# Layer 2's context product in two terms instead of three, and the image columns taken from a wider value product

## The chip, the cores and the metric

The kernel runs on one core of a Trainium2 chip, as one launch. The metric is the device time of one execution in microseconds; the time of a version is the median of its runs. Matrix products run on TensorE (PE), which reads SBUF and writes to PSUM, eight banks of 128 x 512 floats. VectorE (DVE), ScalarE (ACT) and GpSimd (POOL) do the elementwise work, each with a queue of its own that is worked off in order. SyncE (SP) issues most of the transfers, ScalarE some.

## The reference

Two attention layers follow each other on a sequence of 16 batches x 256 positions x 320 channels, 20 heads of 16 channels. Each layer has a context of 256 tokens x 512 channels; the last four tokens are image tokens. Layer 2 is the one that matters here (252 text tokens, 4 image tokens):

```
probs_t  = softmax(q k_t^T * scale)                # text attention, b h s t
text_out = probs_t v_t
qsem     = probs_t @ text_ehs                      # b h s e, 512 wide
qsem     = qsem / max(|qsem|, 1e-12)
ip_n     = ip_ehs / max(|ip_ehs|, 1e-12)
sem      = qsem @ ip_n^T                           # b h s 4
probs_ip = softmax((q k_ip^T) * scale + 0.5*sem) * spatial_mask
out      = (text_out + probs_ip v_ip) @ W_out + b_out + residual
```

The 512 wide `qsem` is never formed. With the context c of a batch, the length of `qsem` is p^T (c c^T) p for a row p of probabilities, and its product with an image token is p^T (c c_image^T). So per batch the kernel needs the product of the context with itself (252 x 252) and of the context with its four image columns.

## The kernel before, in words

**Numbers in two halves.** TensorE's operands are rounded (`float32r`). Where more accuracy is wanted, a value is stored as a high half (rounded) and a low half (the rest), and `prod` (L205) adds three products for each of four 128-channel slices: high by high, high by low, low by high. That is 12 matrix products for one result. `ct(s, k)` is slice k of a batch's context, s = 0 high, s = 1 low, in the buffers `cta`; ScalarE makes the high half and GpSimd the low half (both in `halves`, L147 and L148).

**Layers and slots.** Layer 1 takes slots 0 to 79, layer 2 slots 80 to 159, five slots (groups of four heads) for each batch; a slot of layer 2 takes about 11 us. `slot1` writes out the fixed work of a slot: scores for the maxima (`S`, L780), turned scores (`T`, L775) and their exponentials (`P`, L788), ScalarE's halved and rounded copy of P (`ctb`, L806), GpSimd's remainder (`wt`, L807), the product of the context blocks with the rounded probabilities (`norm1`, L816, bank `X`), VectorE's product of that with the remainder (L817), and `attend1` (L825 with the values `v1t`, L828 with the sums for the length). `settle1` (L870 to L874) turns the result on VectorE.

**Tasks between the fixed work.** Everything that is done once a batch is a generator. `task` gives it due times in slots, and `fill` runs the next step of whichever task is due first, at three points of a slot (0.33, 0.67, 1.0). For batch b, with n = 80 + 5b:
- `keys1` (k1, n-7 to n-4.67): loads the context, makes its halves, and the keys.
- `tokens1` (t1, n-3.67, n-3, n-2.67, n-2.33): two value products of 320 columns (`wC`), then two context products of 256 columns. Text tokens are covered by two tiles of 128 that overlap by four; t = 0 is the first tile, t = 1 starts at token 124 (`DUP`), and `tmask` zeroes the four duplicates.
- `open1` (o1): splits the residual (`hq`, L517 to L519), queries (L528, L536, L537), their product with the image keys.
- `image_softmax` (i1): the softmax over the image tokens, small steps that alternate between GpSimd, VectorE and ScalarE. It begins with a power on GpSimd (L894); `z` (L912) and `rs` (L914) end it, and VectorE turns `rs` (L921).
- `close1` (c1): three image products (L931), added on VectorE (L932), the split `ho`, the output projection (L528).

`tokens1` fills two things: `v1t`, for each head 16 value columns, a column of ones and four image columns (17 to 20), and `G`, seven blocks of 128 x 128 for `norm1`: block 0 is the high half of tile 0 by tile 0 and block 4 its remainder, block 1 the high half of tile 0 by tile 1, blocks 2, 5, 3 and 6 what tile 1 gives. `norm1` adds blocks 0, 2, 4, 5 for the first result and 1, 3, 6 for the second; block 5 is doubled ahead of that (L495).

**What sets the order.** TensorE's instructions stand in the order in which the code issues them. Those of the other engines are ordered by the build's own scheduler, so a change in one step can reorder them around it. PSUM: `X` banks serve `prod`, `norm1`, the maxima and the projections in turn, and a product that needs a bank waits until the engine that reads it out is done. `buf` gives SBUF buffers from fixed rings by name.

Of the kernel before, what the change touches and what calls it, by code (L numbers as in the profile page):

```python
# [9 lines left out]
FR = mybir.dt.float32r  # L10
# [8 lines left out]
H = 20  # L19
# [29 lines left out]
def xattn2(  # L49
# [39 lines left out]
    def bank(tag="X"):  # L89
        return ps.tile([128, 512], F32, tag=tag, name=tag, bufs=BANKS[tag])  # L90
# [3 lines left out]
        return ps.tile([128, 1024], F32, tag="S", name="S", bufs=1).rearrange("p (h t) -> p h t", h=4)  # L94


    words, slots = {"ctb": 1024, "cta": 1024, "raw": 512, "rawc": 512, "kb": 1152, "si": 256, "mt": S, "mx": 2, "kst": 4 * S, "rs": 2 * S, "P": 4 * S}, {}

    def buf(tag, shape, dtype=F32, bufs=1, name=None):
        if tag in ("wB", "wD", "vr", "raw"):  # L100
# [308 lines left out]

    def weights6():  # L410
        cip = w1["cip"]
        w1["v"] = yield from weights(wv1_d, "wC", None, 0.3, "rawc")
        wvi1 = yield from weights_by_column(wvi1_d, 0.3, "rawc")
        vip = buf("rawc", [128, 512], bufs=2, name="vip")[:BI, :CP]
        for m in range(3):
            ms = slice(m * 128, m * 128 + 128)
            vp = bank()[:BI, :128]
            prod(vp, lambda s, k: cip[:, s, k], lambda s, k: wvi1(s, k, ms), 4)
            nc.vector.tensor_copy(vip[:, ms], vp)
            yield  # L420
        ind1 = buf("M", [2, 2, S], FR, bufs=SIZES["M"], name="ind")
        nc.scalar.activation(ind1, ident[:2, :2].unsqueeze(2).to_broadcast([2, 2, S]), AF.Copy, scale=-1.0)
        w1["ind"] = ind1
        dma(kmask, kmask_d.rearrange("(m p) c -> p m c", p=128))
        dma(vipd, vip)
        for i in range(2):
            v = buf("wD", [128, 2, 640], bufs=2, name="v1t")
            nc.gpsimd.memset(v, 0.0)
            nc.vector.memset(vcols(v, V1W)[:, 0, :, 16], 1.0)
            nc.vector.tensor_scalar_add(vcols(v, V1W)[:, 1, :, 16], vcols(v, V1W)[:, 1, :, 16], tmask[:, 2:3])  # L430
            v1t.append(v)
        yield
# [17 lines left out]
            nc.vector.memset(w1["mhalf"], -0.5)  # L450
            nc.gpsimd.memset(w1["pip"], 0.0)

    ct1 = {}

    def keys1(b):
        ct = ct1[b] = yield from context(b, 1, 0.3)
        for m in range(3):
            ms = slice(m * 128, (m + 1) * 128)
            kst = buf("kst", [128, 2, 2, S], FR, bufs=SIZES["KST"]).rearrange("p s b t -> p (s b t)")
            kst = kst[:, : 2 * S].rearrange("p (s b t) -> p s b t", s=2, b=1)  # L460
            kp = bank()[:, :T1]
            prod(kp, lambda s, k: w1["k"](s, k, ms), lambda s, k: ct(s, k)[:, :T1], 4)
            halves(kst[:, 0, 0, :T1], kst[:, 1, 0, :T1], kp)
            nc.gpsimd.tensor_copy(kst[:, :, 0, T1:], f(kip[:, :, m, 4 * b : 4 * b + 4]))
            keys_out(kd[1][b], m, kst)
            yield

    def tokens1(b):
        ct = ct1[b]
        V, G = v1t[b % 2], gmt[b % 2]  # L470
        vc = vcols(V, V1W)
        for t, lo, sc in ((0, 0, 1.0), (1, DUP, tmask[:, 2:3])):
            vp = bank()[:, :320]
            prod(vp, lambda s, k: ct(s, k)[:, lo : lo + 128], w1["v"], 4)
            nc.scalar.activation(vc[:, t, :, 0:16], vp.rearrange("p (h d) -> p h d", d=D), AF.Copy, scale=sc)
            yield
        rnb = rn[:, 4 * b : 4 * b + 4].unsqueeze(1).to_broadcast([128, H, NIP])
        for t, lo in ((0, 0), (1, DUP)):
            g = bank()[:, :S]
            prod(g, lambda s, k: ct(s, k)[:, lo : lo + 128], ct, 4)  # L480
            ip = g[:, T1:S].unsqueeze(1).to_broadcast([128, H, NIP])
            if t == 0:
                nc.vector.tensor_mul(vc[:, 0, :, 17:21], ip, rnb)
                nc.scalar.copy(G[:, 0, :], g[:, 0:128])
                nc.scalar.copy(G[:, 1, 4:], g[:, 128:T1])
                nc.vector.tensor_sub(G[:, 4, :], g[:, 0:128], f(G[:, 0, :]))
            else:
                tm = tmask[:, 2:3]
                nc.vector.scalar_tensor_tensor(vc[:, 1, :, 17:21], ip, tm, rnb, op0=ALU.mult, op1=ALU.mult)
# [5 lines left out]
                nc.vector.tensor_scalar_mul(G[:, 5, :], f(G[:, 5, :]), 2.0)  # L495
                nc.vector.scalar_tensor_tensor(
                    G[:, 6, 4:], g[:, 128:T1], tm, f(G[:, 3, 4:]), op0=ALU.mult, op1=ALU.subtract
                )
            yield
        return V, G  # L500

# [520 lines left out]
    for b in range(B):  # L1022
        n = NS + 5 * b
        task(("k1", b), shifted(n, -7, -6.67, -6.33, -5.67, -5, -4.67), lambda b=b: keys1(b), ("w2",), *([("t1", b - 1)] if b else []), *([("w4", 1)] if b > 2 else []))
        task(("t1", b), shifted(n, -3.67, -3, -2.67, -2.33), lambda b=b: tokens1(b), ("k1", b), ("w3", b % 2))
# [159 lines left out]
```

## Time and profile before

| | us |
|---|---|
| median of 3 runs | 1624.44 |
| lowest, highest | 1620.82, 1625.23 |
| span of the profiled execution, first to last instruction | 1631.7 |
| a batch of layer 2 in the profile | 55.0 |

| engine | busy us | share of the span |
|---|---|---|
| TensorE, products | 1540.0 | 94% |
| TensorE, weight loads (beside the products) | 1235.5 | 76% |
| VectorE | 1215.7 | 75% |
| GpSimd | 1188.4 | 73% |
| ScalarE | 828.8 | 51% |

The profile is one execution with the hardware profiler. No other time is given for it than its span, which is 7.3 us longer than the median of the runs. A row of the timeline has the start, the duration of the group (or of its members together), engine, line, operation, output and inputs, the shape and, in brackets, the engine's idle time before it and what ended it. Products of TensorE are pipelined: the duration of a group runs to the end of its last one, and the next group starts before that, so the cost of a group is the distance to the next start.

### The profile page before, as it was taken

To read this page: it belongs to the slowest core of one execution; us is meant where nothing else is said; L and a number is where in the kernel's file an instruction comes from. 1 tells how busy PE (TensorE), PEld (TensorE's weight loads), DVE (VectorE), ACT (ScalarE), POOL (GpSimd) and SP (SyncE) were. 2 spreads that over 40 slices of the span, in tenths; PEclk is the share of its full clock that TensorE was granted. 3 is DMA by queue.
4 is the path that set the end of the run, shared out by engine and by line. 5 is a ranking of instruction groups with operands and counts; after the bars stand their busy time and mean duration, and the time that the engine had idled before them with its cause. 6 is when DMAs were issued, how large, how long until landed. Compare 5 with 4: busy or idle time off the path is not lost.

```text
span 1631.7 us, 36363 instructions
## 1 busy us (share of the span) xinstructions
PE 1540.0 (94%) x13306; PEld 1235.5 (76%) x13306; DVE 1215.7 (75%) x2410; ACT 828.8 (51%) x1797; POOL 1188.4 (73%) x1147
## 2 busy tenths in 40 slices
PE   7899999999999899789999999999999999999996
PEld 6777878788878787577777777777777777777765
DVE  5467777677777677868877787878777887777785
ACT  5344545445454545435555555545554555555462
POOL 3358787878787867767688668766876787678776
PEclk9799999999999999799999999999999999999998
DMA  7767676667777675666424332433344243423301
GB/s 219 201 202 205 202 203 202 190 207 199 208 199 207 177 210 165 162 191 178 144 74 130 114 125 89 133 120 112 101 126 128 88 125 114 139 81 106 112 26 44
DMA packets 235741, 243.06 MB, mean 149 GB/s; under 512 B 19050, under 2 KB 219468, under 8 KB 235564
## 3 DMA queue, kind: packets, MB, share of 16 engines
q1 hardware_dynamic: 233356, 239.44, 49.8%
q8 instruction: 106, 1.74, 0.5%
q10 hardware_dynamic: 2208, 1.30, 0.3%
q14 instruction: 71, 0.58, 0.1%
HBM read 116.78 MB, written 88.18 MB: 126 GB/s over the span
## 4 chain that ended last, share of the span: by engine, by line
PE 55%; DVE 13%; DMA 10%; POOL 9%; ACT 4%; issue 3%; SPq 3%; ACTq 0%; POOLq 0%; DVEq 0%
PE X L205 15%; PE X L816 12%; PE X L528 7%; PE P L709 5%; PE P L825 3%; DMA qs<-mt 3%; POOL P L682 3%; PE S L652 3%; PE P L828 3%; DMA qs<-qd 3%; PE T L775 3%; SPq L82 2%; PE T L676 2%; DVE wt L817 2%; DVE ho L518 2%
## 5 line engine op out<-in xcount | busy, mean ns | idle before, releaser
L682 POOL TENSOR_TENSOR P<-P,rs 128x512 f32<-128x512 f32 x320 | 413.4, 1313 | 159.5 <-ACT P L679 159.2
L807 POOL TENSOR_TENSOR wt<-P,ctb 128x512 f32<-128x512 f32 x320 | 422.3, 1335 | 93.0 <-ACT ctb L806 91.3
L816 PE MATMUL X<-ctb,gm 128*128 128x512 f32 x1120 | 330.4, 413 | 2.1 <-DVE wt L817 1.1
L679 ACT ACTIVATE P<-T 128x512 f32<-128x512 f32 x320 | 176.1, 595 | 222.1 <-PE T L676 111.8
L806 ACT ACTIVATE ctb<-P 128x512 fp32r<-128x512 f32 x320 | 195.6, 631 | 98.3 <-PE X L816 91.5
L816 PEld LDWEIGHTS X<-ctb,gm 128*128 128x128 f32 x1120 | 189.2, 188 | 72.3 <-issue 15.6
L817 DVE TENSOR_TENSOR wt<-X,wt 128x512 f32<-128x512 f32 x320 | 218.2, 683 | 33.9 <-PE X L816 28.4
L781 DVE TENSOR_REDUCE mn<-S 128x4 fp32r<-128x1008 f32 x160 | 191.8, 1199 | 48.3 <-PE S L780 48.2
L788 ACT ACTIVATE P<-T 128x512 f32<-128x512 f32 x320 | 173.7, 595 | 64.3 <-PE P L825 48.3
L654 DVE TENSOR_REDUCE mn<-S 128x4 fp32r<-128x716 f32 x160 | 142.5, 891 | 0.0
L709 PE MATMUL P<-P,vr 128*32 128x256 f32 x1920 | 132.1, 409 | 3.3 <-DVE mx L581 2.3
L676 PE MATMUL T<-qs,ks 127*128 127x256 f32 x640 | 112.3, 295 | 22.6 <-DMA qs<-mt 10.7
L652 PE MATMUL S<-ks,qs 125*128 125x256 f32 x640 | 118.4, 309 | 3.7 <-DVE mn L654 2.5
L652 PEld LDWEIGHTS S<-ks,qs 125*128 125x128 f32 x640 | 89.3, 196 | 40.6 <-issue 35.0
L528 PE MATMUL X<-ho,wF 128*128 128x256 f32 x768 | 112.8, 290 | 6.3 <-DVE ho L518 3.0
L528 PE MATMUL X<-hq,wE 128*128 128x256 f32 x768 | 111.5, 289 | 7.1 <-ACT hq L517 3.3
L894 POOL TENSOR_TENSOR r<-u,rs 128x40 f32<-128x40 f32 (+2 forms) x17 | 108.7, 6393 | 7.7 <-DVE u L891 7.6
L676 PEld LDWEIGHTS T<-qs,ks 127*128 127x128 f32 x640 | 92.8, 198 | 28.0 <-DVE tmp L726 11.6
L528 PEld LDWEIGHTS X<-ho,wF 128*128 128x128 f32 x768 | 103.2, 194 | 12.6 <-DVE ho L518 4.7
L528 PEld LDWEIGHTS X<-hq,wE 128*128 128x128 f32 x768 | 103.5, 195 | 11.7 <-ACT hq L517 3.7
L205 PE MATMUL X<-cta,wA 128*128 128x252 f32 (+1 forms) x720 | 100.9, 286 | 7.3 <-ACT wA L147 5.7
L205 PEld LDWEIGHTS X<-cta,wA 128*128 128x128 f32 x720 | 94.1, 195 | 12.5 <-ACT wA L147 5.9
(197 smaller groups left out, 2813.6 us busy)
## 6 DMA issues: line engine op xcount, KB each, us to landing
qd<-q SPq DMA_DIRECT2D x96, 384.0 KB
qs<-tph SPq DMA_DIRECT2D x64, 308.0 KB
kd<-kst SPq DMA_DIRECT2D x73, 256.0 KB
rawc<-in_cT_dram SPq DMA_DIRECT2D x60, 256.0 KB
qs<-qd SPq DMA_DIRECT2D x80, 192.0 KB
ks<-kd SPq DMA_DIRECT2D x80, 192.0 KB
ks<-kd SPq DMA_DIRECT2D x160, 96.0 KB
qs<-qd SPq DMA_DIRECT2D x160, 96.0 KB
```

The lines of the kernel that those rows point to most:

```text
L205: last = mm(out, lhs(a, k), rhs(b, k), start=i == 0, stop=i == len(terms) - 1)
L528: mm(pp, w(s, k, slice(m * 128, (m + 1) * 128)), a[:, t], start=i == 0, stop=i == len(terms) - 1)
L652: mm(sp[:, h], Q[: XROW + T0, h, t * 128 : (t + 1) * 128], K[: XROW + T0, h], start=True, stop=True)
L676: mm(st[p][:, j], K[:KS0, 2 * p + j, t * 128 : (t + 1) * 128], Q[:KS0, 2 * p + j], start=True, stop=True)
L679: exp = anchor(nc.scalar.activation(pt, st[p], AF.Exp, scale=SCALE))
L682: anchor(nc.gpsimd.tensor_mul(pt, pt, rs[:, t : t + 1].to_broadcast([128, 2, S])))
L709: mm(pv[32 * s : 32 * s + 32, o : o + S], v[:, vt, h : h + 32], P[k, s // 2][:, t, s % 2], start=vt < 2, stop=vt != 1,)
L781: anchor(nc.vector.tensor_reduce(maxes[k + 2][:, t], sp[:, :, :T1], axis=AX.X, op=ALU.max))
L806: nc.scalar.activation(R[k, u][:, t], P[k, u][:, t], AF.Copy, scale=0.5)
L807: anchor(nc.gpsimd.tensor_sub(W[k, u][:, t], P[k, u][:, t], f(R[k, u][:, t])))
L816: mm(yp, gm[:, gb], R[k, u][:, kt], start=i == 0, stop=i == len(blocks[n]) - 1)
L817: nc.vector.tensor_mul(W[k, u][:, n], yp, W[k, u][:, n])
```

## The change

- The context product becomes two terms. For each slice the stationary operand is the high half in both; the moving operands are the high half and the doubled low half, 252 columns. That is 8 products instead of 12 for each of the two tiles. Twice high by low is not symmetric, but p^T (A + A^T) p = 2 p^T A p.
- The doubled low halves (`two`, in buffers `tph`) are made on ScalarE at the end of `keys1`, four instructions of 128 x 252.
- The image columns come from the value product: `wC` has four more columns for each slice and half, which GpSimd fills with the image columns of the context (four copies of 128 x 8 a batch). The value products have 324 columns, and the two VectorE products for columns 17 to 20 of `v1t` move to the value steps.
- Of tile 0 by tile 1 the remainder is kept (`across`, VectorE), turned on TensorE in a fifth step of `tokens1`, due at n-2, into free columns of the bank of the second context product, and added to block 5 (VectorE). Block 5's doubling goes.

```diff
 def weights6():
-        w1["v"] = yield from weights(wv1_d, "wC", None, 0.3, "rawc")
+        wv = w1["wv"] = buf("wC", [128, 2, 4, H * D + NIP], FR)
+        parts = [(wv1_d[k * 128 : (k + 1) * 128], wv[:, 0, k, : H * D], wv[:, 1, k, : H * D]) for k in range(4)]
+        yield from in_turn(parts, 0.3, "rawc")
...
 def keys1(b):
...
+        two = [buf("tph", [128, 2, S], FR, bufs=2, name="two") for i in range(2)]
+        twice = doubled[b] = lambda k: two[k // 2][:, k % 2, :T1]
+        for k in range(4):
+            nc.gpsimd.tensor_copy(wv[:, :, k, H * D :], f(ct(slice(None), k)[:, :, T1:]))
+        for k in range(4):
+            nc.scalar.activation(twice(k), f(ct(1, k)[:, :T1]), AF.Copy, scale=2.0)
+        yield
...
 def tokens1(b):
-            vp = bank()[:, :320]
-            prod(vp, lambda s, k: ct(s, k)[:, lo : lo + 128], w1["v"], 4)
+            vp = bank()[:, : H * D + NIP]
+            prod(vp, lambda s, k: ct(s, k)[:, lo : lo + 128], lambda s, k: wv[:, s, k], 4)
...
         for t, lo in ((0, 0), (1, DUP)):
-            g = bank()[:, :S]
-            prod(g, lambda s, k: ct(s, k)[:, lo : lo + 128], ct, 4)
-            ip = g[:, T1:S].unsqueeze(1).to_broadcast([128, H, NIP])
+            g = bank()
+            for i, k in enumerate(k for k in range(4) for j in range(2)):
+                rhs = twice(k) if i % 2 else ct(0, k)[:, :T1]
+                mm(g[:, :T1], ct(0, k)[:, lo : lo + 128], rhs, start=i == 0, stop=i == 7)
             if t == 0:
+                across = buf("sp", [128, 128], bufs=2, name="across")
+                nc.gpsimd.memset(across[:, :4], 0.0)
...
+                nc.vector.tensor_sub(across[:, 4:], g[:, 128:T1], f(G[:, 1, 4:]))
             else:
...
-                nc.vector.tensor_scalar_mul(G[:, 5, :], f(G[:, 5, :]), 2.0)
...
+                yield
+                nc.tensor.transpose(g[:, S : S + 128], across, ident)
+                nc.vector.tensor_add(G[:, 5, :], g[:, S : S + 128], f(G[:, 5, :]))
             yield
...
-        task(("t1", b), shifted(n, -3.67, -3, -2.67, -2.33), ...
+        task(("t1", b), shifted(n, -3.67, -3, -2.67, -2.33, -2), ...
```

More of the change, by code (lines that the diff above doesn't have):

```diff
@@ L94, in scores @@
         return ps.tile([128, 1024], F32, tag="S", name="S", bufs=1).rearrange("p (h t) -> p h t", h=4)
-    words, slots = {"ctb": 1024, "cta": 1024, "raw": 512, "rawc": 512, "kb": 1152, "si": 256, "mt": S, "mx": 2, "kst": 4 * S, "rs": 2 * S, "P": 4 * S}, {}
+    words, slots = {"ctb": 1024, "cta": 1024, "raw": 512, "rawc": 512, "kb": 1152, "si": 256, "sp": 128, "wC": 2 * 4 * (H * D + NIP), "mt": S, "mx": 2, "kst": 4 * S, "rs": 2 * S, "P": 4 * S}, {}
     def buf(tag, shape, dtype=F32, bufs=1, name=None):
@@ L451, in weights3 @@
             nc.gpsimd.memset(w1["pip"], 0.0)
-    ct1 = {}
+    ct1, doubled = {}, {}
     def keys1(b):
```

26 lines of the change are left out of this document (17 added, 9 removed).

## The prediction

> **What bounds the kernel now.** I read the page's busy shares first, then the chain that ended last, then the busy time by stretches, then the waits, and last the timeline of one batch of layer 2, engine by engine. On the page (busy us, share of the span, instructions):
>
> ```profile
> PE 1540.0 (94%) x13306; PEld 1235.5 (76%) x13306; DVE 1215.7 (75%) x2410; ACT 828.8 (51%) x1797; POOL 1188.4 (73%) x1147
> ```
> ```profile
> PE 55%; DVE 13%; DMA 10%; POOL 9%; ACT 4%; issue 3%; SPq 3%; ACTq 0%; POOLq 0%; DVEq 0%
> ```
>
> TensorE is busy 94% of the span, and 55% of the chain is its work. The changed code runs once a batch in layer 2, whose batches are five slots long. Two stretches of 55 us, 500 us apart (columns: the stretch, its length, then PE, PEld, DVE, ACT, POOL busy, granted clock, DMA share, GB/s):
>
> ```profile
> 910.00:965.00 55.00, 54.29 (x471) 41.83 (x467) 43.07 (x78) 29.78 (x62) 40.86 (x39) 1.00 0.37 115
> ...
> 1460.00:1515.00 55.00, 54.31 (x475) 41.78 (x471) 43.02 (x79) 29.74 (x63) 40.85 (x39) 1.00 0.32 98
> ```
>
> A batch of layer 2 takes 55.0 us and TensorE is busy 54.3 of them at full granted clock. So this stage is TensorE's, almost. The "almost" decides this case, and stands in the timeline of TensorE:
>
> ```profile
> 948.83 0.70 PE L931 MATMUL X<-rs,rs 128*128 128x256 f32 x2 [0.56 <-DVE wt L817]
> ...
> 956.91 1.20 PE L816 MATMUL X<-ctb,gm 128*128 128x512 f32 x4 [0.15 <-DVE wt L817]
> ```
> ```profile
> PE X L931 <- DVE wt L817: 6.5, 12, 0.6
> ```
>
> In each batch TensorE stops 0.56 us ahead of the third small image product of `close1` (L931), and 0.15 us some 8 us later; the row of waits (between 860 and 1515 us) shows the first in 12 of 12 batches. These are the only stops of TensorE between 910 and 966 us. The first ends when VectorE has emptied a PSUM bank (L817 releases it). VectorE's rows ahead of it:
>
> ```profile
> 944.18 0.45 DVE L921 STREAM_TRANSPOSE rs<-rs 128x256 f32<-128x256 f32 x1 [1.36 <-POOL rs L914]
> 944.55 0.41 DVE L870 STREAM_TRANSPOSE nt<-P 128x256 f32<-128x256 f32 x1
> ...
> 945.44 0.68 DVE L817 TENSOR_TENSOR wt<-X,wt 128x512 f32<-128x512 f32 x1
> 946.04 0.41 DVE L537 TENSOR_TENSOR q<-X,q 128x256 fp32r<-128x256 f32 x1
> ...
> 946.98 1.20 DVE L781 TENSOR_REDUCE mn<-S 128x4 fp32r<-128x1008 f32 x1
> 948.09 0.68 DVE L817 TENSOR_TENSOR wt<-X,wt 128x512 f32<-128x512 f32 x1
> ```
>
> VectorE stood idle 1.36 us for GpSimd's `rs` (L914), and then worked without a gap until L817 from 948.09 released the product at 948.83. GpSimd in turn:
>
> ```profile
> 923.20 6.77 POOL L894 TENSOR_TENSOR r<-u,rs 128x40 f32<-128x40 f32 x1 [0.47 <-DVE u L891]
> ...
> 938.19 2.81 POOL L807 TENSOR_TENSOR wt<-P,ctb 128x512 f32<-128x512 f32 x2 [0.46 <-ACT ctb L806]
> 940.96 0.27 POOL L912 TENSOR_TENSOR z<-z,mk 128x40 f32<-128x40 f32 x1
> 941.18 1.28 POOL L807 TENSOR_TENSOR wt<-P,ctb 128x512 f32<-128x512 f32 x1
> 942.42 1.30 POOL L518 TENSOR_TENSOR hq<-xq,hq 128x512 fp32r<-128x512 f32 x1
> 943.67 0.48 POOL L914 TENSOR_TENSOR rs<-a,z 128x160 f32<-128x160 f32 x1
> 944.10 1.31 POOL L148 TENSOR_TENSOR cta<-rawc,cta 128x512 fp32r<-128x512 f32 x1
> ...
> 950.75 2.98 POOL L807 TENSOR_TENSOR wt<-P,ctb 128x512 f32<-128x512 f32 x2
> ```
>
> The power (6.77 us) blocks GpSimd's queue, and the backlog behind it runs until `rs` is done at 944.15. Its only gap on the way is 0.46 us at 938.19, for ScalarE. **So two paths are almost equally long:** TensorE's own work, and GpSimd from the power to `rs`, then VectorE. A saving on TensorE before 938 us counts only as far as the second path also gets shorter.
>
> **TensorE's part.** Rows of the removed and changed products and of what starts right behind each:
>
> ```profile
> 911.05 1.54 PE L205 MATMUL X<-cta,wA 128*128 128x252 f32 x12
> 912.43 0.86 PE L816 MATMUL X<-ctb,gm 128*128 128x512 f32 x3
> ...
> 921.47 1.93 PE L205 MATMUL X<-wC,cta 128*128 128x320 f32 x12
> 923.24 0.86 PE L816 MATMUL X<-ctb,gm 128*128 128x512 f32 x3
> ...
> 932.98 1.59 PE L205 MATMUL X<-cta 128*128 128x256 f32 x12
> 934.41 0.86 PE L816 MATMUL X<-ctb,gm 128*128 128x512 f32 x3
> 935.20 0.51 PE L775 MATMUL T<-qs,ks 50*128 50x256 f32 x4
> ...
> 936.89 1.57 PE L205 MATMUL X<-cta 128*128 128x256 f32 x12
> 938.30 0.86 PE L816 MATMUL X<-ctb,gm 128*128 128x512 f32 x3
> ```
>
> Twelve context products of 256 columns take 1.43 us (932.98 to 934.41) and 1.41 us. Twelve of 252 columns take 1.38 us (911.05 to 912.43), so the new eight cost 0.92 us: 0.51 and 0.49 saved, 1.00 in all. Value products: twelve of 320 columns take 1.77 us, 0.46 ns a column; four columns more are 0.02 us, twice 0.04. The turned block is a new TensorE operation. Nearest is the 77-row transpose of layer 1 (durations min/median/max in ns):
>
> ```profile
> L593 PE MATMUL X<-ident,sp x32: 270/272/497, 31.7 to 665.2; 128*77 128x128 f32 x32
> ```
>
> I take its 270 ns for the bound above and 0.06 us (a 128-column product at 0.46 ns) below. Net 0.69 to 0.90 us saved a batch. If TensorE alone set the time, 16 batches would give 11 to 14 us.
>
> **The other engines.** On GpSimd: four copies of 8 elements, each like the first of these rows, and a tiny memset:
>
> ```profile
> 911.64 0.19 POOL L464 CAST kst<-kip 128x8 fp32r<-128x8 f32 x1 [0.76 <-DMA kd<-kst]
> ...
> 937.26 0.47 POOL L904 TENSOR_TENSOR a<-a,m 128x160 f32<-128x160 f32 x1
> ```
>
> In the built program the copies stand well ahead of the value products (two after `rs`, two between L807's subtractions of the next slot), so 0.8 us of GpSimd lies beside TensorE's work; it would cost something only if it pushed `rs`, and it stands behind it. The memset (taken at 0.1 us) stands ahead of `rs`. On VectorE the doubling of block 5 goes and a subtraction and an addition of one block come:
>
> ```profile
> 940.97 0.34 DVE L495 TENSOR_SCALAR gm<-gm 128x128 fp32r<-128x128 f32 x1
> ```
>
> So about 0.34 us net, in stretches where VectorE waits anyway (that 1.36 us); the two image-column products only move to the value step. On ScalarE four doublings of 128x252 come; the last row below is a cast of that size:
>
> ```profile
> 935.76 1.10 ACT L788 ACTIVATE P<-T 128x512 f32<-128x512 f32 x2
> 936.72 0.86 ACT L517 CAST hq<-xq 128x768 fp32r<-128x768 f32 x1
> 937.45 0.67 ACT L806 ACTIVATE ctb<-P 128x512 fp32r<-128x512 f32 x1
> ...
> 955.42 0.37 ACT L147 CAST kst<-X 128x252 fp32r<-128x252 f32 x1 [2.47 <-PE X L205]
> ```
>
> That is 4 x 0.37 = 1.5 us on an engine busy 29.8 of 55. But they read the low half that GpSimd writes (L148, `cta`), and in the built program two of them stand ahead of the query cast L536 in ScalarE's queue: ScalarE will wait for `cta`, with L536, L806 and the next exponentials queued behind. I check that below. The turn adds a wait to TensorE: it writes into the bank of the second context product, so it waits for VectorE's last reading of it (block 6, now L496), with the next scores T and S queued behind it. Its cover is worked out at the end of the next part.
>
> **The GpSimd path after the change.** The built program changes the order. Before: three L807, `z` (L912), `hq` (L518), `rs`, with the subtraction of the maximum (L904) done earlier; VectorE has `rs` ahead of the transposition of P. After: L807, L904, two L807, `hq`, memset, `z`, `cta`, `rs`; VectorE takes the transposition, two small steps and one L817 first and `rs` after them. So `cta` (1.25 us from start to next start) and L904 (0.47) come into the path, and 1.36 us of waiting is used for work.
>
> Step by step. The first saved 0.51 us less V's 0.04 brings the scores T from 935.20 to 934.73. Their 0.51 us end at 935.24, so the exponentials start at 935.27 instead of 935.76, `hq`'s cast and L806 follow, and GpSimd's L807 starts at 937.70 instead of 938.19: 0.49 passed on, and GpSimd is idle ahead of it as it is now, L904 having moved behind it. From there at start-to-start durations: L807 three times 1.24 (941.18 to 942.42), L904 0.47, `hq` 1.25, memset 0.1, `z` 0.22, `cta` 1.25, `rs` 0.48: 7.49, so `rs` is done at 945.19. VectorE: `rs` 0.37, L817 0.60, L537 0.34, the reduction L781 1.11, L817 0.60, with 0.1 for two hand-overs 3.12: the third product starts at 948.30. It was 948.83. Gain 0.53 us a batch. ScalarE's check: `cta` ends 944.71, two doublings 945.45, L536 945.85; VectorE wants it at 946.2. It is hidden with 0.35 us to spare. TensorE's check: without a stop it would have been at the third product at 948.27 (948.83 less 0.56); 0.69 saved makes that 947.58, so the wait for the turn may last 0.72 us and cost nothing; beyond that each tenth counts.
>
> From L931 on the sequence is as before (VectorE's `ho`, then the L816 of 956.91), so 0.53 us is the batch's gain. Fourteen batches have their context product in the steady stage (from 800 to 1570 us at 55 us each): 14 x 0.53 = 7.4 us. The first two fall in the change-over between the layers, where I have no chain; bounds 0 and 1.4, I take 0.6. Sum: 8.0 us. Against the profiled execution: 1631.7 - 8.0 = 1623.7 us of span. That execution's span is 7.3 us above the median of the runs shown; the same 8.0 from the median gives 1616.4 us. What a measurement of this kernel tells from no change is 0.3%, 4.9 us.
>
> **A rule of the skill at this place.** The same operation on the same shape:
>
> ```profile
> 938.12 0.48 DVE L519 SCALAR_TENSOR_TENSOR hq<-hq,tmask,xq 128x256 fp32r<-128x256 f32 x1
> ...
> 952.51 1.50 DVE L519 SCALAR_TENSOR_TENSOR ho<-ho,tmask,hT 128x256 fp32r<-128x256 f32 x1
> ```
>
> It took 0.48 us while GpSimd was idle, and 1.50 while two L807 ran (2.98 us for the two, against 1.24 each elsewhere). The Trainium skill, page "SBUF — State Buffer", section "Who interferes with whom", says that a VectorE instruction with two SBUF inputs and a GpSimd instruction that reads SBUF exclude each other for the whole instruction. The trace's 1.50 against 0.48 agrees. By that rule the added GpSimd copies speak against the change, but here `ho`, half a microsecond earlier, would meet `cta` and two copies of 0.19 us in place of a second L807, would shorten by up to 1.0 us, and the stop of 0.15 us at 956.91 would go; that is the second case below. The sum by the rows alone stays 1616.4.
>
> **Rivals.**
> - *Forecast:* the GpSimd path shortens by 0.53 us a batch. Between half of it and 0.7: 1612 to 1621. Chance 0.48.
> - *TensorE stays the bound.* The VectorE pair at 951 to 954 us meets shorter GpSimd work, the 0.15 us go as well: 0.68 x 14 + 0.6 = 10.1, and TensorE's own bound allows 11 to 14: about 1613 us. For it: TensorE is busy 54.3 of 55. Against: the path above. Chance 0.14.
> - *The gain is swallowed.* If GpSimd's run starts at 938.19 as now (another operand of L806 or L807 is late), the third product starts at 948.79, 0.04 earlier than now: 1624 us, no change. For it: `cta` and L904 now stand ahead of `rs`. Chance 0.22.
> - *Slower: the longer GpSimd run collides with VectorE.* Five passes of 128x512 (three L807, `hq`, `cta`) now stand between ScalarE's release and `rs`. At 1.49 us each, as in the row from 950.75, instead of 1.24 they take 1.25 us more: the third product at 949.55, 0.72 later than now, 14 x 0.72 = 10: 1634.5 us. It decides from 0.53 us more, 0.11 a pass. For it: L807 from 938.19 took 1.40 each, 0.3 us more for the two. Against: the in-place VectorE pass on block 5 that read only SBUF is gone. Chance 0.16.
>
> **How the numbers follow.** Faster by over 0.3% (below 1619.6) are nine tenths of the forecast's case and all of the second: 0.43 + 0.14, with a rounding 0.58. Within 0.3%: the rest of the first and the swallowed gain, 0.26. Slower: 0.16. The range: 1609 takes in TensorE's bound of 14 us and a little more; 1630 takes in the swallowed gain and the collision up to half its price. About 0.06 lies below and 0.12 above.
>
> **What would show it.** Right: eight context products at 0.92 us; the stop ahead of the third image product still there, 0.7 to 0.9 us together with a stop at the turned block, and ended by VectorE; VectorE still waiting for `rs`, but with the transposition of P ahead of it; batches of 54.5 us. Wrong: batches of 54.3 or less with no stop at L931 (TensorE bounds); batches of 55 or more with `rs` done after 945.7 in the same counting; a ScalarE gap for `cta` that ends later than L536 is wanted; a stop of TensorE at the turned block of more than 1 us.

## The result and the profile after

The changed kernel takes 1618.63 us (median of 6 runs, 1612.52 to 1623.3). The kernel before took 1623.53 us beside it (median of 6, 1620.82 to 1626.7). The two medians differ by 4.9 us (0.9970). The ratio on record, which is not the quotient of these two medians, is 0.9956 with a 95% interval of 0.9938 to 0.9975: faster by 0.44%, about 7 us. The forecast was 1616.4 us, 8.0 us less than before.

The profiled execution of the changed kernel took 1612.52 us, the lowest of the six, with a span of 1610.7 us, which is 21.0 us less than the span before. Most of that can't be put down to the change. The first value product of layer 2 starts at 711.06 us in place of 723.59, so 12.5 us lie ahead of it, in layer 1, whose own code is the same in both kernels. In the eleven other profiles of this study the same point lies between 713.7 and 720.9, so it scatters by several us. (The four profiles of the kernel before and its variants have it at 717.4 to 723.6, the nine others at 711.1 to 720.9; a small part of the change's there can't be excluded.) From that point to the end it is 899.6 in place of 908.1 us, **8.5 us less**. All that follows is counted from there, or by the batch. The page (busy us, share, instructions) and the chain that ended last:

```profile
PE 1518.9 (94%) x13194; PEld 1218.1 (76%) x13194; DVE 1212.2 (75%) x2426; ACT 847.1 (53%) x1861; POOL 1195.7 (74%) x1227
PE 63%; DMA 9%; DVE 8%; POOL 8%; ACT 4%; issue 3%; SPq 1%; ACTq 0%; POOLq 0%; DVEq 0%
```

TensorE's share of the chain rose from 55% to 63% and VectorE's fell from 13% to 8%. That fits less waiting of TensorE for VectorE, but a share of the chain doesn't show where. TensorE's rows of the value product, ten batches apart, give the length of a batch:

```profile
909.15 1.95 PE L205 MATMUL X<-wC,cta 128*128 128x324 f32 x12
...
1452.56 1.95 PE L205 MATMUL X<-wC,cta 128*128 128x324 f32 x12
```

(1452.56 - 909.15) / 10 is 54.34 us. Before, the same row came at 921.47 and 1472.56, 55.11 by this count, with one batch of 55.55 among nine of about 55.05. TensorE's timeline in the batch from 909.15, the new rows and its stops:

```profile
924.12 0.28 PE L502 MATMUL X<-cta 128*128 128x252 f32 x1
...
925.04 0.86 PE L839 MATMUL X<-ctb,gm 128*128 128x512 f32 x3
...
927.20 0.33 PE L520 MATMUL X<-ident,sp 128*128 128x128 f32 x1 [0.17 <-DVE gm L516]
927.46 0.50 PE L798 MATMUL T<-qs,ks 50*128 50x256 f32 x4
...
935.93 0.70 PE L954 MATMUL X<-rs,rs 128*128 128x256 f32 x2 [0.41 <-DVE wt L840]
```

Eight products of 252 columns (the first is shown) take 0.92 us (924.12 to 925.04). The turned block stands in the stream from 927.20 to 927.46, after a stop of 0.17 us. The stop ahead of the third image product (L931 before, L954 now) went from 0.56 to 0.41 us. The stop of 0.15 us some 8 us later is gone. The waits of TensorE between 860 and 1500 us (in total, times, longest) show the stop at the image product in 10 of 12 batches (in the other two TensorE stops 0.31 and 0.18 us one product later) and the one at the turned block in all 12:

```profile
PE X L954 <- DVE wt L840: 4.2, 10, 0.4
PE X L520 <- DVE gm L516: 2.1, 12, 0.2
```

GpSimd's queue behind the power (now L917), and VectorE behind `rs` (L937):

```profile
910.89 6.77 POOL L917 TENSOR_TENSOR r<-u,rs 128x40 f32<-128x40 f32 x1 [0.47 <-DVE u L914]
...
925.36 1.29 POOL L830 TENSOR_TENSOR wt<-P,ctb 128x512 f32<-128x512 f32 x1 [0.37 <-ACT ctb L829]
926.62 0.46 POOL L927 TENSOR_TENSOR a<-a,m 128x160 f32<-128x160 f32 x1
927.05 2.52 POOL L830 TENSOR_TENSOR wt<-P,ctb 128x512 f32<-128x512 f32 x2
929.53 1.30 POOL L541 TENSOR_TENSOR hq<-xq,hq 128x512 fp32r<-128x512 f32 x1
...
931.05 1.30 POOL L148 TENSOR_TENSOR cta<-rawc,cta 128x512 fp32r<-128x512 f32 x1
932.30 0.48 POOL L937 TENSOR_TENSOR rs<-a,z 128x160 f32<-128x160 f32 x1
```
```profile
932.81 0.45 DVE L944 STREAM_TRANSPOSE rs<-rs 128x256 f32<-128x256 f32 x1 [0.89 <-POOL rs L937]
933.18 0.65 DVE L840 TENSOR_TENSOR wt<-X,wt 128x512 f32<-128x512 f32 x1
933.76 0.41 DVE L560 TENSOR_TENSOR q<-X,q 128x256 fp32r<-128x256 f32 x1
934.09 1.19 DVE L804 TENSOR_REDUCE mn<-S 128x4 fp32r<-128x1008 f32 x1
935.20 0.67 DVE L840 TENSOR_TENSOR wt<-X,wt 128x512 f32<-128x512 f32 x1
```

The five passes of 128x512 still take 1.23 to 1.26 us from start to start (`hq`'s to the small memset at 930.76), now with `cta` among them ahead of `rs`. VectorE still waits for `rs` (0.89 us) and then works without a gap until L840 releases the third image product.

The change-over between the layers went the other way. From the first value product to that of the third batch it is 89.96 us (711.06 to 801.02); before it was 89.27 (723.59 to 812.86). TensorE's stops at the turned block there:

```profile
724.49 0.33 PE L520 MATMUL X<-ident,sp 128*128 128x128 f32 x1 [2.23 <-DVE gm L516]
767.03 0.33 PE L520 MATMUL X<-ident,sp 128*128 128x128 f32 x1 [0.49 <-DVE gm L516]
818.56 0.33 PE L520 MATMUL X<-ident,sp 128*128 128x128 f32 x1 [1.63 <-DVE gm L516]
```

These two profiles show the loss at its smallest. Three more profiles run the code of the kernel before up to this point (before_nopow, before_rs and before_rs2, below): 87.9 to 88.0 us. In the one profile of 89.27 the granted clock fell to 0.79 and 0.78 in the two stretches of 4 us from 720 us. Two more run the code of the changed kernel (after_nopow, after_rs): 91.9 and 91.4 us, with a lower clock behind the first stop at the turned block (last section). So the change-over lost 0.7 us in this pair of profiles, and 2 to 4 us when one or both sides are taken from the others.

### The profile page after: what moved, and what is told of

It reads as the page before. It is cut to its first block, busy times and chain, and to the rows that moved or that the text cites. A ratio compares the mean times of both kernels' runs of the same rounds, so it can differ in the third digit from the quotient of the medians.

```text
span 1610.7 us, 36262 instructions
## 1 busy us (share of the span) xinstructions
PE 1518.9 (94%) x13194; PEld 1218.1 (76%) x13194; DVE 1212.2 (75%) x2426; ACT 847.1 (53%) x1861; POOL 1195.7 (74%) x1227
## 4 chain that ended last, share of the span: by engine, by line
PE 63%; DMA 9%; DVE 8%; POOL 8%; ACT 4%; issue 3%; SPq 1%; ACTq 0%; POOLq 0%; DVEq 0%
PE X L205 16%; PE X L839 13%; PE X L551 7%; PE P L732 6%; PE P L848 4%; PE S L675 4%; PE T L798 3%; PE P L851 3%; PE T L699 3%; POOL wt L830 2%; DMA kd<-kst 2%; DMA qs<-qd 2%; DMA qs<-mt 2%; PE S L803 2%; DVE wt L840 1%
## 5 line engine op out<-in xcount | busy, mean ns | idle before, releaser
L830 POOL TENSOR_TENSOR wt<-P,ctb 128x512 f32<-128x512 f32 x320 | 419.0, 1324 | 95.0 <-ACT ctb L829 93.6
L840 DVE TENSOR_TENSOR wt<-X,wt 128x512 f32<-128x512 f32 x320 | 218.4, 683 | 18.9 <-PE X L839 13.4
L732 PE MATMUL P<-P,vr 128*32 128x256 f32 x1920 | 128.7, 404 | 0.9 <-DVE mx L604 0.9
L917 POOL TENSOR_TENSOR r<-u,rs 128x40 f32<-128x40 f32 (+2 forms) x17 | 108.7, 6394 | 7.4 <-DVE u L914 7.2
```

The lines of the kernel that those rows point to most:

```text
L732: mm(pv[32 * s : 32 * s + 32, o : o + S], v[:, vt, h : h + 32], P[k, s // 2][:, t, s % 2], start=vt < 2, stop=vt != 1,)
L830: anchor(nc.gpsimd.tensor_sub(W[k, u][:, t], P[k, u][:, t], f(R[k, u][:, t])))
L840: nc.vector.tensor_mul(W[k, u][:, n], yp, W[k, u][:, n])
```

## The experiments

The theory (A): in the kernel before, two paths were nearly equal, TensorE's work and GpSimd's backlog from the power to `rs` with VectorE behind it; the change shortened both. The rival (B): TensorE's work alone counts, and its stops are incidental. Each ratio is to runs of the kernel before on the same chip. "Batch" is a tenth of the time between value products ten batches apart, and "layer 2" the time from the first value product to the end, both from one profiled execution.

| kernel | median us | ratio to before | 95% interval | first value product, ten batches apart | batch us | layer 2 us |
|---|---|---|---|---|---|---|
| before | 1623.53 | | | 921.47, 1472.56 | 55.11 | 908.1 |
| changed | 1618.63 | 0.9956 | 0.9938 to 0.9975 | 909.15, 1452.56 | 54.34 | 899.6 |
| images_only | 1616.78 | 0.9944 | 0.9930 to 0.9959 | 911.01, 1456.93 | 54.59 | 901.3 |
| twelve | 1623.27 | 0.9984 | 0.9971 to 0.9998 | 915.02, 1466.15 | 55.11 | 909.4 |
| before_nopow | 1610.45 | 0.9906 | 0.9890 to 0.9922 | 912.73, 1456.18 | 54.35 | 892.9 |
| after_nopow | 1603.40 | 0.9863 | 0.9841 to 0.9885 | 915.71, 1452.48 | 53.68 | 889.7 |
| before_rs | 1625.72 | 0.9995 | 0.9977 to 1.0013 | 921.72, 1467.70 | 54.60 | 906.0 |
| before_rs2 | 1620.08 | 0.9967 | 0.9948 to 0.9987 | 916.44, 1462.62 | 54.62 | 900.7 |
| after_rs | 1625.09 | 0.9989 | 0.9970 to 1.0009 | 920.39, 1469.21 | 54.88 | 908.3 |
| combined | 1622.57 | 0.9987 | 0.9969 to 1.0004 | 915.07, 1463.51 | 54.84 | 904.6 |
| turn_later | 1612.54 | 0.9915 | 0.9892 to 0.9938 | 910.89, 1452.69 | 54.18 | 895.3 |
| turn_cta | 1617.72 | 0.9952 | 0.9934 to 0.9971 | 914.01, 1461.33 | 54.73 | 902.9 |
| no_turn | 1616.00 | 0.9931 | 0.9907 to 0.9955 | 917.86, 1461.66 | 54.38 | 898.4 |

**Without the power** (before_nopow and after_nopow, one word each, which makes the image probabilities other numbers):

```diff
-        pool.tensor_tensor(r, u, w1["mhalf"].rearrange("p (f s) -> p f s", f=NG)[:, gs], op=ALU.pow)
+        pool.tensor_tensor(r, u, w1["mhalf"].rearrange("p (f s) -> p f s", f=NG)[:, gs], op=ALU.mult)
```

> The kernel before with GpSimd's power (6.77 us, once a batch in layer 2) replaced by a multiplication of the same operands, so the image probabilities of layer 2 are other numbers; the order of instructions is as before. Theory A: without the backlog `rs` comes early, the stop of 0.56 us ahead of the third image product goes in every batch, and with it perhaps the 0.15 us later: 54.3 to 54.5 us a batch in place of 55.04, 7 to 10 us less, 1613 to 1616. Theory B (TensorE's work alone sets the batch, and the stops are made up elsewhere): batches of 55.0, 1623. The last batch, which has nothing behind it, may give up to 6 us more under either theory, so the batches of the steady stage decide.

> The same replacement of the power in the changed kernel (image probabilities of layer 2 other numbers). Theory A: the stop of 0.41 us at the third image product goes, the one of 0.17 us at the turned block stays: batches of 53.9 in place of 54.34 us, 14 x 0.41 = 5.7 us less, about 1613. Against the kernel before without the power the batch is then shorter by TensorE's net saving alone, 0.6 to 0.8 us. Theory B: batches of 54.3, no change but in the last batch. A third reading (VectorE has become the bound of that stretch and not GpSimd): the stop keeps over 0.3 us, with VectorE busy without a gap ahead of it.

One batch of each, busy time by stretches (stretch, its length, then PE, PEld, DVE, ACT, POOL, granted clock, DMA share, GB/s):

```profile
967.34:1021.65 54.31, 54.20 (x469) 41.76 (x467) 42.68 (x78) 29.79 (x62) 34.65 (x39) 1.00 0.34 105
```
```profile
969.45:1023.15 53.70, 53.52 (x461) 41.17 (x460) 43.10 (x80) 31.08 (x66) 35.15 (x44) 1.00 0.36 118
```

In the first, TensorE's list of waits between 860 and 1500 us is empty; in the second it holds only the 0.18 us at the turn. So without GpSimd's power the stop at the third image product goes in both kernels, and the batch loses 0.76 and 0.66 us. That is theory A; B is out. (That VectorE just meets less GpSimd work is a rival here; before_rs, below, takes no work away. Of the 15 us that before_nopow gains in all, 4.3 are the last batch: 104.1 to 99.8 us from the last value product to the end.) Together the pair gives what the change is worth to TensorE alone: 54.35 - 53.68 = 0.67 us a batch, turn and its stop included. TensorE's busy time in the two batches shown falls by 0.68 us. In the kernels with the power the batch is shorter by 0.77, or by 0.71 from a usual batch of before (55.05): as much as TensorE's whole saving came through there. I read this as the second path being shortened as well, since TensorE still stops for it.

**Only the image columns moved** (images_only):

```diff
-            for i, k in enumerate(k for k in range(4) for j in range(2)):
-                rhs = twice(k) if i % 2 else ct(0, k)[:, :T1]
-                mm(g[:, :T1], ct(0, k)[:, lo : lo + 128], rhs, start=i == 0, stop=i == 7)
+            prod(g[:, :T1], lambda s, k: ct(s, k)[:, lo : lo + 128], lambda s, k: ct(s, k)[:, :T1], 4)
...
-                nc.tensor.transpose(g[:, S : S + 128], across, ident)
-                nc.vector.tensor_add(G[:, 5, :], g[:, S : S + 128], f(G[:, 5, :]))
+                nc.vector.tensor_scalar_mul(G[:, 5, :], f(G[:, 5, :]), 2.0)
```

(The doubled low halves and `across` are left out with them.)

> The changed kernel with the context product left at three terms (twelve products of 252 columns, block 5 doubled by VectorE as before; no doubled low, no turned block), so only the image columns move to the wider value product. TensorE's work is that of the kernel before within 0.05 us a batch (24 products four columns narrower, 24 four columns wider). In the built program GpSimd has `rs` ahead of the last L807 and of `hq`, two passes of about 1.25 us earlier than in the kernel before. Theory A (GpSimd's backlog behind the power sets the stop ahead of the third image product): the stop of 0.56 us a batch goes, batches of 54.4 to 54.5 us in place of 55.04, about 7 to 9 us faster than before (1615 to 1617), with no work taken from TensorE. Theory B (the time gained by the change is the TensorE work saved): no change from before, 1623, batches of 55.0.

```profile
965.67:1020.24 54.57, 54.52 (x468) 41.90 (x467) 43.70 (x79) 29.82 (x62) 41.54 (x43) 1.00 0.36 117
```

1616.78 us, a ratio of 0.9944, batches of 54.59 and not one listed stop of TensorE: theory A's numbers, the batch 0.1 us longer. TensorE does the work of the kernel before, and the kernel still gains about what the whole change did (the intervals overlap). GpSimd's `rs` has moved ahead of two passes of 1.25 us: VectorE takes it 20.1 us into the batch in place of 22.7. With it the batch is 0.52 us shorter (55.11 to 54.59; 0.46 from a usual batch); TensorE's saving, where no second path stands in its way, is 0.67. The edit also moves the image columns and VectorE's work on them, so that the order does it is shown only by before_rs and before_rs2, which change nothing else.

**Twelve products again** (twelve), all else of the change kept:

```diff
-            for i, k in enumerate(k for k in range(4) for j in range(2)):
-                rhs = twice(k) if i % 2 else ct(0, k)[:, :T1]
-                mm(g[:, :T1], ct(0, k)[:, lo : lo + 128], rhs, start=i == 0, stop=i == 7)
+            for i, k in enumerate(k for k in range(4) for j in range(3)):
+                rhs = twice(k) if i % 3 == 1 else ct(0, k)[:, :T1]
+                mm(g[:, :T1], ct(0, k)[:, lo : lo + 128], rhs, start=i == 0, stop=i == 11)
```

> The changed kernel with four more products in each context product (high by high twice), so TensorE does twelve of 252 columns a tile again, with all else of the change kept (doubled lows, turned block, copies). The sums are other numbers. TensorE's work is 0.92 us a batch more than in the changed kernel. In the built program `rs` also stands ahead of the last L807, `hq` and `cta` on GpSimd. Theory A: TensorE's own work then bounds, the stop of 0.41 us at the third image product goes, and the batch is 54.34 + 0.92 - 0.41 = 54.85 us: 14 x 0.51 + 2 x 0.9 = 9 us over the changed kernel, 1627. Theory B (TensorE's work alone counts, the stop stays or is made up elsewhere): 16 x 0.92 = 14.7 us over it, 1633, batches of 55.26.

```profile
969.85:1024.70 54.85, 54.67 (x470) 42.05 (x468) 43.46 (x79) 30.85 (x66) 41.58 (x44) 1.00 0.33 104
```

The usual batch is 54.85 us, theory A's number (B: 55.26). The total, 1623.27 us, is 4.6 us over the changed kernel's median (4.5 by the two ratios), less than A's 9 and far from B's 14.7. In the profile layer 2 is 9.8 us longer, and 2.7 of that come from one batch of 57.51 us, which the last section takes up.

**`rs` earlier by order alone.** Since images_only had `rs` early, I tried the order by itself, on both kernels (the first three added lines in after_rs only):

```diff
+        low = order(eng.tensor_sub(lo, src, f(hi)))
+        if eng is nc.gpsimd and "rs" in w1:
+            queued(low, w1["rs"])
...
+        low = order(eng.tensor_sub(hl[:, 3:5], src[:, 0:2], f(hl[:, 0:2])))
+        if tag == "hq" and "rs" in w1:
+            queued(low, w1["rs"])
...
+        w1["rs"] = pool.tensor_mul(by_group(pi), a, b4(z4))
```

> The kernel before with one order added and nothing else: in layer 2 GpSimd's `hq` subtraction (L518, 1.25 us) is queued behind `rs` (L914) in place of ahead of it. No engine has less work. Theory A: `rs` comes 1.25 us earlier, the stops of 0.56 and 0.15 us a batch go as they went without the power, 54.3 to 54.5 us a batch in place of 55.05: 8 to 10 us off, 1614 to 1617. Theory B (the gain without the power came from the missing 6.8 us of GpSimd's work itself, which shares memory ports with VectorE, not from `rs` coming earlier): batches of 54.9 to 55.1, 1624.

> The changed kernel with the same order: `hq` and the `cta` subtraction queued behind `rs` on GpSimd. Theory A: `rs` about 2.5 us earlier, the stop of 0.41 us at the third image product goes, batches of 53.7 to 53.9 in place of 54.34 as without the power: 6 to 9 us below the changed kernel, 1610 to 1613. The difference to the kernel before in the same order is then what the change is worth to TensorE alone: 0.6 to 0.7 us a batch. Theory B: 54.3 us a batch. A cost that could eat it: `cta` is written 0.5 us later, and ScalarE's doublings and what is queued behind them with it.

In before_rs the stops go and the batch is 54.60 us, 0.1 above what A said and 0.45 below a usual one of before. The total doesn't move, because in the first batch `hq` waits for the first `rs`:

```profile
832.29 1.86 PE L530 MATMUL X<-hq,wE 128*128 128x256 f32 x7 [2.91 <-POOL hq L518]
```

The batch around it took 58.44 us in place of 53.56. With the order only from the second batch on, that is avoided (the other lines of before_rs stay):

```diff
-        w1["rs"] = pool.tensor_mul(by_group(pi), a, b4(z4))
+        rs = pool.tensor_mul(by_group(pi), a, b4(z4))
+        if b:
+            w1["rs"] = rs
```

> The kernel before with `hq` queued behind `rs` as in the earlier run, but only from the second batch of layer 2 on, since in the first batch that order made TensorE wait 2.9 us for `hq` and the batch took 5 us longer. Theory A (the order takes the stops away, 0.45 us a batch): no long batch, steady batches of 54.6 in place of 55.05, about 6 us below the kernel before, 1617 to 1620. Theory B: the long batch comes back in the second batch, where `rs` is as late for the first time, and the total is that of the kernel before.

Measured: 1620.08 us, 0.9967, layer 2 900.7 in place of 908.1, batches of 54.62, no long one. TensorE now stops for `hq` in 7 of 12 batches, for 0.2 us at most. So a change of one queue position gains 0.33% (0.13 to 0.52) on the kernel before, with no work removed.

On the changed kernel the same order failed: batches of 54.88. Its waits:

```profile
PE X L555 <- POOL hq L543: 4.5, 12, 0.4
PE X L843 <- DVE wt L844: 2.5, 11, 0.2
PE X L522 <- DVE gm L518: 2.1, 12, 0.2
```

The stop at the image product is gone, and TensorE stops at the projection (L555) for `hq`, 12 times in 12 batches. My expectation costed what `rs` gains and did not ask who waits for the `hq` that moved behind it.

**The turned block.** In turn_later it has a bank of its own and comes later (its due time n-2 goes); in no_turn the three removed lines below are left out with nothing in their place.

```diff
-                yield
-                nc.tensor.transpose(g[:, S : S + 128], across, ident)
-                nc.vector.tensor_add(G[:, 5, :], g[:, S : S + 128], f(G[:, 5, :]))
+                def turn():
+                    tp = bank()[:, :128]
+                    nc.tensor.transpose(tp, across, ident)
+                    nc.vector.tensor_add(G[:, 5, :], tp, f(G[:, 5, :]))
+                later(0.6, turn)
```

> The changed kernel with the turned block taken 0.6 slots later into a PSUM bank of its own, behind the next scores T and S in place of ahead of them (four due times for the task in place of five). Theory A: TensorE's stops at the turn go (0.17 us a batch, and 2.23, 0.49 and 1.63 us in the change-over between the layers), and T, from which GpSimd's path starts, comes 0.43 us earlier (0.17 of stop and 0.26 of the turn): the third image product 0.4 us earlier with a stop of about 0.15 left, 14 x 0.4 + up to 4 = 6 to 10 us below the changed kernel, 1609 to 1613. Rival (stops that are made up later cost nothing, in the change-over above all): 14 x 0.17 = 2.4 us or less, 1616 to 1619.

> The changed kernel without the turned block and its addition, so the half-term of one context block is left out of the sums. Theory A: TensorE loses 0.26 us of the turn and 0.17 of the stop a batch, both ahead of T, so GpSimd's path also starts 0.43 us earlier: batches of 53.9 to 54.0 in place of 54.34, and no stops at the turn in the change-over: 6 to 9 us below the changed kernel, 1610 to 1612; against the later turn (54.15) that leaves the turn itself 0.2 us a batch. Rival (the turn lies beside the wait that follows at the third image product): batches of 54.3, 1617.

no_turn has batches of 54.33 us (54.38 with one of 55.00 among the ten), as the changed kernel has: in the steady stage the turn and its stop cost nothing. The stop ahead of the third image product grows from 0.41 to 0.55:

```profile
PE X L951 <- DVE wt L837: 6.5, 12, 0.6
```

That is the rival of this expectation, and my reason was wrong: GpSimd's path starts at a T ahead of the second context product, not at the one behind the turn, so nothing on it moved. In the change-over the turn does cost: 89.03 us from the first to the third batch without it, 89.96 with it (90.6 to 91.9 in three other profiles with it).

turn_later is the fastest version that leaves nothing out, 1612.54 us, a ratio of 0.9915 (0.9892 to 0.9938), and 895.3 us in layer 2, 4.3 less than the changed kernel. 1.3 of that is the change-over (88.70 us). In the steady batch (54.18) it isn't the earlier T that I expected: VectorE takes `rs` 23.6 to 23.7 us into the batch in both kernels, but none of the third product's stop is left, and TensorE stops one product later:

```profile
PE X L843 <- DVE wt L844: 4.3, 12, 0.4
```

The pass of VectorE that ends the stop is the one behind the reduction in both; it ends 26.7 us into the batch in the changed kernel and 26.9 here. One more bank taken in each batch shifts which bank each later product gets. That this is what moved the stop I read from the order alone; it wasn't tried by itself.

**Two attempts at more.** combined puts together both orders (`hq` and `cta` behind `rs`), the later turn, and the doublings queued behind the last key cast; turn_cta has the later turn and only `cta` behind `rs`, by the lines shown above. The doublings' line in combined:

```diff
-            nc.scalar.activation(twice(k), f(ct(1, k)[:, :T1]), AF.Copy, scale=2.0)
+            queued(nc.scalar.activation(twice(k), f(ct(1, k)[:, :T1]), AF.Copy, scale=2.0), cast)
```

> The changed kernel with both: `hq` and `cta` behind `rs` on GpSimd, the turn later in a bank of its own, and ScalarE's four doublings queued behind the last key cast, so that ScalarE no longer waits about 2 us for `cta` with the query cast behind it. Theory A: no stop of TensorE is left in a batch, which is then TensorE's work alone, 53.5 to 53.6 us (53.70 without the power, less the 0.18 at the turn), and up to 4 us less in the change-over: 13 us or so below the changed kernel, about 1606. Rival: the four doublings in a row (1.5 us) push L806's cast on ScalarE, GpSimd starts later, and a stop comes back: 54.0 or more, 1612.

> The changed kernel with the turn later in its own bank, and on GpSimd only the `cta` subtraction behind `rs` (`hq` stays ahead of it, since TensorE waits for `hq` when it is moved). In the built program ScalarE's query cast then stands ahead of the doublings. Theory A: `rs` 1.25 us earlier than with the later turn alone, the stop of 0.37 us left there goes, batches of 53.7 to 53.9 in place of 54.15: 4 to 6 us below the kernel with the later turn, 1606 to 1609. Rival (VectorE, whose reductions and `ho` pair stand between, sets the stop): batches of 54.1, 1612.

Both missed. In combined TensorE waits for `hq`, as in after_rs:

```profile
PE X L560 <- POOL hq L548: 8.9, 12, 1.0
```

In turn_cta VectorE takes `rs` 1.1 us earlier than in turn_later and the third product doesn't wait, but TensorE stops some 8 us later, at the place of the 0.15 us stop of before, and the batch grew to 54.73:

```profile
PE X L845 <- DVE wt L846: 4.4, 12, 0.4
```

The part of the reason that I could trace stands in the last section: with `cta` behind `rs` GpSimd's passes after it come later against VectorE, whose `ho` then waits longer for them.

## Why the prediction was right, and which terms were off

- **The products.** 0.92 us for eight, as worked out. The turn cost 0.26 us in the stream, the upper end taken from the 77-row transposes; 252 columns were no surprise. By the rows that makes 1.00 less 0.04 less 0.26, 0.70 us a batch, and TensorE's busy time in the pair without the power fell by 0.68 (54.20 to 53.52): the lower end of 0.69 to 0.90.
- **The GpSimd path.** Counted from the power's start, the prediction had L807 at 14.50 us, `rs` done at 21.99, the third product at 25.10. Measured: 14.47 (925.36), 21.89 (932.78), 25.04 (935.93). The gain at that point, predicted 0.53 us, was 25.63 - 25.04 = 0.59. The cost of `cta` and L904 ahead of `rs`, and VectorE's use of its former wait, came as summed. The stops came smaller than the sign that was named: 0.41 and 0.17 us are 0.58 together, not 0.7 to 0.9.
- **The covers.** ScalarE waited for `cta` as foreseen and VectorE had `q` without a gap:

```profile
932.38 0.72 ACT L476 ACTIVATE tph<-cta 128x252 fp32r<-128x252 f32 x2 [1.97 <-POOL cta L148]
933.01 0.35 ACT L559 CAST q<-X 128x256 fp32r<-128x256 f32 x1
```

  The turn's wait was free in the steady stage, as no_turn shows.
- **What was mis-sized, one:** the steady batch. The prediction let 0.53 us through and gave the vanishing of the later 0.15 us stop to another case. It vanished. VectorE's `ho` subtraction ahead of it took 1.34 us before (first row) and 0.78 after (second; the third is the row behind it):

```profile
951.24 1.34 DVE L518 TENSOR_TENSOR ho<-hT,ho 128x512 fp32r<-128x512 f32 x1 [0.29 <-ACT ho L517]
```
```profile
938.28 0.78 DVE L541 TENSOR_TENSOR ho<-hT,ho 128x512 fp32r<-128x512 f32 x1 [0.23 <-ACT ho L540]
938.99 1.50 DVE L542 SCALAR_TENSOR_TENSOR ho<-ho,tmask,hT 128x256 fp32r<-128x256 f32 x1
```

  Before, this row began 0.49 us after a GpSimd pass had started (950.75), now 1.07 us after one (937.21); the last section shows why that matters. The row that the prediction named, 1.50 us, took 1.50 us again (938.99). So a batch gained 0.7 us (55.05 to 54.34). From the fourth value product to the sixteenth it is 651.76 us in place of 661.18: 9.4 us where 12 x 0.53 would be 6.4; 0.5 of it is the one long batch of before.
- **What was mis-sized, two:** the change-over. I took a gain of 0.6 us between bounds of 0 and 1.4, without a row for the turn's wait there. It lost 0.7 us to the third batch and 0.3 more to the fourth (53.56 to 53.88), at stops of 2.23 and 1.63 us that the prediction's own list names as a sign against it. Below nothing was not in the bounds, and the wait that the change added should have put it there.
- In this pair of profiles 9.4 less 1.0 is 8.4, and 8.5 was measured against 8.0: the two errors nearly cancel, so the sum is better than its terms, by luck. With the change-over as in the other profiles (a loss of 2 to 4 us to the third batch in place of 0.7) the same count gives an estimate of 5 to 7 us, which lies nearer to the 4.9 us between the medians and the 7 us of the ratio.
- **The rivals.** Collision: refuted, the passes took 1.23 to 1.26 us. Swallowed gain: refuted, L830 started 0.5 us earlier. TensorE alone: refuted by the stop that stayed and by the runs without the power, though its second half, the 0.15 us, came true, and with it its price: 0.68 us a batch lies nearer to the measured 0.71 than the forecast's 0.53. (Its 10.1 us make 1614.3 us; the text's 1613 leans on TensorE's own bound.)

## What to carry to other kernels

A stop of half a microsecond in each batch on an engine that is busy 94% can mean, as here, that a second path is as long; ask what leads to it, because moving one instruction in that queue may gain as much as removing work. Before an instruction goes behind another, list who waits for it, in the first iteration too, where its new forerunner comes latest. A term for the change-over between two stages needs its own rows: a wait that is covered in the steady stage stood open there.

## What the runs showed of the hardware

**A stop can cost more than its length.** In twelve, TensorE stopped once for 1.42 us, and then the granted clock was below 1 (column after the five busy times):

```profile
1044.91 0.33 PE L520 MATMUL X<-ident,sp 128*128 128x128 f32 x1 [1.42 <-DVE gm L516]
```
```profile
1044.00:1048.00 4.00, 3.09 (x33) 1.84 (x37) 3.08 (x7) 1.31 (x3) 4.00 (x5) 0.77 0.30 104
1048.00:1052.00 4.00, 4.00 (x27) 2.60 (x19) 1.70 (x5) 1.47 (x5) 2.08 (x6) 0.80 0.58 185
1052.00:1056.00 4.00, 4.00 (x24) 3.08 (x23) 3.75 (x7) 3.00 (x6) 2.42 (x2) 1.00 0.22 77
```

That batch was 2.66 us longer than its neighbours (57.51 against 54.85). In before_rs, after the 2.91 us for `hq`:

```profile
832.00:836.00 4.00, 3.71 (x16) 2.96 (x18) 0.95 (x2) 1.00 (x2) 0.85 (x2) 0.50 0.40 123
836.00:840.00 4.00, 4.00 (x18) 3.08 (x17) 2.85 (x6) 2.12 (x4) 2.27 (x3) 0.72 0.00 0
```

Not each stop does it: after the 2.23 us and the 1.63 us of the changed kernel the clock stayed at 1.00 in every stretch of 4 us. But after_nopow and after_rs run the same code up to there, with the same first stop of 2.24 us, and behind it the clock fell (after_nopow first, whose stop ends at 730.87; in after_rs it ends at 732.04):

```profile
732.00:736.00 4.00, 4.00 (x36) 2.51 (x34) 1.49 (x2) 1.09 (x2) 2.50 (x2) 0.59 0.19 57
```
```profile
732.00:736.00 4.00, 3.96 (x23) 3.38 (x25) 1.50 (x2) 1.45 (x3) 1.43 (x3) 0.57 0.35 101
```

The Trainium skill, page "TensorE: Matmul & The Clock Gate", Part 1, tells of free-running activity windows of about 3.4 us and a lower clock after an idle one. That the same stop lowered the clock in two profiles and not in a third agrees; that 1.42 us was enough once is less idle time than the page asks for.

**VectorE and GpSimd take turns.** VectorE's `ho` subtraction reads two SBUF operands. In three kernels, in each of 12 batches, it started while GpSimd's pass on `cta` was running:

```profile
937.21 1.30 POOL L148 TENSOR_TENSOR cta<-rawc,cta 128x512 fp32r<-128x512 f32 x1
```
```profile
1101.66 1.29 POOL L148 TENSOR_TENSOR cta<-rawc,cta 128x512 fp32r<-128x512 f32 x1
1102.54 0.95 DVE L545 TENSOR_TENSOR ho<-hT,ho 128x512 fp32r<-128x512 f32 x1 [0.23 <-ACT ho L544]
```
```profile
1106.62 1.28 POOL L148 TENSOR_TENSOR cta<-rawc,cta 128x512 fp32r<-128x512 f32 x1
1107.05 1.40 DVE L547 TENSOR_TENSOR ho<-hT,ho 128x512 fp32r<-128x512 f32 x1 [0.23 <-ACT ho L546]
```

These are the changed kernel (its `ho` is shown above, from 938.28), turn_later and turn_cta. The durations are 0.78, 0.95 and 1.40 us, but the ends lie 0.55, 0.54 and 0.55 us behind the end of `cta` (939.06 to 938.51, 1103.49 to 1102.95, 1108.45 to 1107.90). In all 36 batches the distance is 0.54 to 0.56 us. So VectorE waits for the whole GpSimd instruction and then needs 0.55 us. This is the rule that the prediction weighed, from the Trainium skill, page "SBUF — State Buffer", section "Who interferes with whom", and the trace agrees. It tells why an order on GpSimd that looks free (turn_cta) lengthens VectorE's path: a row's duration on VectorE holds its wait for GpSimd, with no gap shown.

Which of the two starts first decides who waits. In the prediction's row of 0.48 us (938.12) GpSimd was idle only for the first 0.07 us; its pair of passes then took 2.81 us. In twelve the usual batch (first row) has `hq`'s L542 0.13 us ahead of a GpSimd pass (986.55), the long one (second row) 0.33 us behind the start of one (1041.56):

```profile
986.42 0.47 DVE L542 SCALAR_TENSOR_TENSOR hq<-hq,tmask,xq 128x256 fp32r<-128x256 f32 x1
```
```profile
1041.89 1.25 DVE L542 SCALAR_TENSOR_TENSOR hq<-hq,tmask,xq 128x256 fp32r<-128x256 f32 x1
```

Counted from the value product, L542 began 0.6 us later in the long batch, and L516, which releases the turned block, 1.2 us later: that is the stop of 1.42 us in place of 0.18. What made the first 0.6 us was not traced.
